# Edge weights loaded pair by pair, edge attributes in 1 KB rows, and an activation written with a step that restores the order of edges

## The chip, the core and the metric

The kernel runs on one core of one Trainium2 chip. The metric is the device time of one execution in microseconds (us); the lower, the better. The core has five engines that work side by side: TensorE (PE, matrix products; its weight loads are listed as PEld), VectorE (DVE), ScalarE (ACT), GpSimd (POOL) and SyncE (SP), which here issues nearly all plain DMAs. Sixteen DMA engines move the data. In the profile, SPq is SP's queue of instructions.

## What is computed

One layer of graph attention with 12,500 nodes of 128 channels and 400,000 edges, sorted by their destination. The edges' part is what the change touches:

```python
msg_src = node_input @ w_src + b_src
msg_dst = node_input @ w_dst
message = msg_src[edge_src] + msg_dst[edge_dst]
rad_w = silu(silu(edge_scalars @ w1 + b1) @ w2 + b2) @ w3 + b3     # 32 -> 64 -> 64 -> 128
message = message * edge_attr * rad_w                              # edge_attr: one weight per edge
message = message @ w_sep + b_sep
alpha, value = halves of each of 8 heads                           # 16 + 16 channels a head
score = sum(smooth_leaky_relu(alpha) * alpha_dot)                  # one per edge and head
att = softmax of score over the edges of one destination
out = segment_sum(value * att, edge_dst) @ w_proj + b_proj
```

The layer's input is a normalized and rectified `x`, and `x` is added to its output. `edge_scalars` is the input `edge_attr_32` (32 numbers per edge, the *attributes*), and `edge_attr` is the input `edge_weight1` (the *weight* of an edge). All numbers are 32-bit floats.

## The kernel before

**Stages.** A first stage makes the two tables of node messages, `t_src` and `t_dst`, in DRAM. The main stage, `passes`, walks over the edges. A last stage projects the sums and adds `x`. The change lies in `passes` alone.

**Sections and pairs.** The edges are cut into 800 sections of `SEC = 500` (four tiles of `T = 125`), and two consecutive sections make a pair of `PR = 1000`. There are `NP = 400` pairs. One call of `step(k)` does one piece of the work of several pairs at once: loads for pairs ahead, the radial net and the message of pair k, and the sums of the older pair `c = k - LAG`, with `LAG = 12`. The order inside a step is written by hand (`manual_schedule`), and each engine takes its own instructions in that order.

**The radial net.** `load_e(g)` brings the attributes of four pairs (500 KB) into the tile `e_t`, every fourth step. Edge number j·125 + p of the group goes to partition p, column block j, so each DMA row is one edge's 32 floats, 128 bytes. `e_T` transposes a pair on PE, and ACT copies the result to `eT`. `mlp1` and `mlp2` are matrix products, each followed by a SiLU on ACT (L740, L755). Blocks on the diagonal of the weights let one product treat two sets of edges. `mlp3` (L769) has PE form the 128 radial factors of the 1000 edges in PSUM, and DVE adds the bias and multiplies with the edge weights, giving two tiles `rad` (L772).

**The weights.** `load_w(g)` broadcasts the weights of two pairs (2000 floats) to all 128 partitions, 1000 KB in all, into `w_b` with two buffers. It is called at every even step, for the pairs k + 2 and k + 3.

**The message.** `message` adds, on PE, the transposed gathered rows `gs` (L782) and a product of a one-hot matrix with `m3` (L788). `m3` holds `md`, the rows of `t_dst` that the pair needs, split into three bf16 parts by `split_md`; the first part is a cast on ACT (L704), and `md` is loaded by `load_md(k + 3)` (L698). DVE multiplies by `rad` to get `mT` (L793). `alphas` (L797, L799, L801), `scores` and the softmax come after that. The rows `gs` are gathered by POOL (L718), eight indirect DMAs a step.

**The sums.** `sums(c)` leaves the sums of pair c in `ob` (ACT, L896). `store(c, f)` writes 63 rows of them to `agg` in DRAM at a place that is read from a register (L903). Because those places are not known beforehand, each store to `agg` waits until the store before it has landed.

**SP's queue.** SP issues in the order of the calls. In a step this is: `store_win` in one step of four, the first store of pair c - 1, `load_w` in even steps, two `md` loads, in steps with k % 4 == 1 the loads `d_b` (L687, the local destination numbers of four pairs, 500 KB) and `e_t` (L681), and then the second store of pair c - 1. Traffic of scores and of the softmax comes at the end of some steps.

Of the kernel before, what the change touches and what calls it, by code (L numbers as in the profile page):

```python
# [21 lines left out]
F32 = mybir.dt.float32  # L22
# [3 lines left out]
ALU = mybir.AluOpType  # L26
# [4 lines left out]
P = 128  # L31
C = 128
H = 8
RAD = 32
# [11 lines left out]
T = 125  # L46
TS = 4
SEC = T * TS
W = 64
PR = 2 * SEC  # L50
# [6 lines left out]
def gnn_kernel(ctx: ExitStack, tc: tile.TileContext, a: dict, out: bass.AP):  # L57
    nc = tc.nc
    x, src, dst = a["x"], a["src"], a["dst"]
    ea, ew = a["edge_attr_32"], a["edge_weight1"]  # L60
# [84 lines left out]
    with tc.tile_pool(name="node", bufs=2) as np_, tc.tile_pool(name="node1", bufs=1) as n1, \  # L145
# [27 lines left out]
        w3, b3 = load("fc_w3", [FC, C]), load("fc_b3", [C, 1])  # L173
# [463 lines left out]
    def passes(w1b, w2b, w3b, b12, w_s, b_s, row, far):  # L637
        src_t = src.rearrange("(s e) -> s e", e=SEC)
        dst_t = dst.rearrange("(s e) -> s e", e=SEC)
        ea_t = ea.rearrange("(g j p) c -> g p j c", j=32, p=T)  # L640
        ew_p = ew.rearrange("(g e) o -> o g e", e=2 * PR)
        with tc.tile_pool(name="wk2", bufs=2) as sp, tc.tile_pool(name="ps", bufs=1, space=PSUM) as pp, \
                tc.manual_schedule(), ExitStack() as held:
            lp = held.enter_context(tc.tile_pool(name="ld", bufs=2))
            prep, e_g, d_g, w_g, md, gath = {}, {}, {}, {}, {}, {}
            eTs, h1s, h2s, ohT, m3, mr, mTs, als, S_all, sms, Ps, Pem, pvx, ohs, accs, Sps, Ms = (
                {} for _ in range(17))
# [29 lines left out]
                prep[u] = (idx, loc)  # L677

            def load_e(g):
                e_g[g] = lp.tile([T, 32, RAD], F32, name="e_t")  # L680
                nc.sync.dma_start(out=e_g[g], in_=ea_t[g])  # L681

            def load_d(g):
# [2 lines left out]
                at = bass.AP(at.tensor, at.offset, [[NP * SEC, 2], [0, W], [1, 4 * SEC]])  # L686
                nc.sync.dma_start(out=d_g[g].rearrange("p k e -> p (k e)"), in_=at)  # L687

            def load_w(g):
                w_g[g] = lp.tile([P, 2, PR], F32, name="w_b")  # L690
                nc.sync.dma_start(out=w_g[g].rearrange("p k e -> p (k e)"),
                                  in_=ew_p[:, g, :].to_broadcast([P, 2 * PR]))

            def load_md(k):
                md[k] = lp.tile([P, C], F32, name="md", bufs=4)
                at = [nc.sync.value_load(base[0:1, f, k:k + 1]) for f in range(2)]
                for f in range(2):
                    nc.sync.dma_start(out=md[k][f * W:(f + 1) * W, :], in_=t_dst[ds(at[f], W), :])  # L698
# [23 lines left out]


            def e_T(k):
                ev = e_g[k // 4].rearrange("p (k f t) c -> p k f (t c)", k=4, f=2)
                pe = pp.tile([P, 2, T], F32, name="m1")
                for g in range(2):
                    nc.tensor.transpose(pe[:, g, :], ev[:, k % 4, g, :], ident[:T, :T])
                eTs[k] = sp.tile([P, 2 * T], F32, name="eT")
                nc.scalar.copy(eTs[k], pe.rearrange("p g e -> p (g e)"))  # L730
# [13 lines left out]
            def mlp2(k):  # L744

                p2 = pp.tile([P, 2, BANK], F32, name="p3")
                h1 = h1s.pop(k)
                for h in range(2):
                    s = slice(h * FC, (h + 1) * FC)
                    for f in range(2):  # L750
                        o = slice(f * FC, (f + 1) * FC)
                        nc.tensor.matmul(p2[o, h, 0:2 * T], w2b[s, o], h1[s, f * 2 * T:(f + 1) * 2 * T],  # L752
                                         start=True, stop=True)
                h2s[k] = sp.tile([P, SEC], F32, name="h2")
                nc.scalar.activation(h2s[k].rearrange("x (q h p) -> x h q p", q=2, h=2),  # L755
                                     p2[:, :, 0:2 * T].rearrange("x h (q p) -> x h q p", q=2),
                                     AF.Silu, bias=b12[:, 1:2], scale=1.0)

# [6 lines left out]
            def mlp3(k):  # L765
                p3 = pp.tile([C, 2, BANK], F32, name="p3")
                for f in range(2):
                    s = slice(f * FC, (f + 1) * FC)
                    nc.tensor.matmul(p3[:, f, 0:SEC], w3b[s, :], h2s[k][s, :], start=True, stop=True)  # L769
                rads = [sp.tile([C, SEC], F32, name="rad", bufs=3) for _ in range(2)]  # L770
                for f in range(2):
                    nc.vector.scalar_tensor_tensor(  # L772
                        rads[f], p3[:, f, 0:SEC], b3, w_g[k // 2][:, k % 2, f * SEC:(f + 1) * SEC],
                        op0=ALU.add, op1=ALU.mult)
                return rads

            def message(k, rads):
                gs = gath[k]
                pm = [pp.tile([C, SEC], F32, name="pm", bufs=2) for _ in range(2)]
                for f in range(2):  # L780
                    for t in range(TS):
                        nc.tensor.matmul(pm[f][:, t * T:(t + 1) * T], gs[:T, f * TS + t, :],  # L782
                                         ident[:T, :T], start=(t == 0), stop=False,
                                         is_transpose=True, skip_group_check=True)
                for j in range(3):
                    for f in range(2):
                        s = slice(f * W, (f + 1) * W)
                        nc.tensor.matmul(pm[f], m3[k][s, j, :], ohT[k][s, :], start=False, stop=(j == 2),  # L788
                                         skip_group_check=True)
                mTs[k] = sp.tile([C, PR], F32, name="mT", bufs=LAG + 1)  # L790
                for f in range(2):
                    s = slice(f * SEC, (f + 1) * SEC)
                    nc.vector.tensor_mul(mTs[k][:, s], pm[f], rads[f])  # L793

            def alphas(k, f):
                pa = pp.tile([C, SEC], F32, name="pa")
# [101 lines left out]
            def store_win(g):  # L898
                nc.sync.dma_start(out=win[4 * g:4 * g + 4].rearrange("k p c -> p k c"), in_=accs[g])
# [5 lines left out]
            def has(k):  # L905
                return 0 <= k < NP
# [5 lines left out]
            def step(k):  # L912
                c = k - LAG
                if has(c - 1):
                    if c % 4 == 0:
                        store_win(c // 4 - 1)
                    store(c - 1, 0)

                if k % 16 == 4 and has(k + 12):
                    prep_load((k + 12) // 16)  # L920
                if k % 2 == 0 and has(k + 2):
                    load_w((k + 2) // 2)
                if has(k + 3):
                    load_md(k + 3)
                if k % 4 == 1 and has(k + 3):
                    load_d((k + 3) // 4)
                if k % 4 == 1 and has(k + 7):
                    load_e((k + 7) // 4)
                if has(k + 4) and (k + 4) % MP == 0:
                    load_sm((k + 4) // MP)  # L930
                if has(c - 1):
                    store(c - 1, 1)
                if 0 <= 2 * k < NZ:
                    for i in range(2 * k, min(2 * k + 2, NZ)):
                        zero(i)
                if k % 16 == 8 and has(k + 8):
                    prep_make((k + 8) // 16)
                if has(k + 4):
                    gather(k + 4)
                if has(k + 1):  # L940
                    split_md(k + 1, 0)
                if has(c):
                    sums_begin(c)
                if has(k):
                    message(k, mlp3(k))
                if has(c):
                    values(c, 0)
                if has(k + 1):
                    split_md(k + 1, 1)
                if has(k):  # L950
                    alphas(k, 0)
                if has(k + 1):
                    split_md(k + 1, 2)
                if has(k + 2):
                    mlp1(k + 2)
                if has(c):
                    values(c, 1)
                if has(k):
                    alphas(k, 1)
                if has(k + 1):  # L960
                    mlp2(k + 1)
                    one_hot_T(k + 1)
                    split_md(k + 1, 3)
                if has(c):
                    sums(c)
                m, r = divmod(k, MP)
                if has(k - MP):
                    if r == 1:
                        softmax_up(m - 1)
                    elif r == 2:  # L970
                        softmax_down(m - 1)
                        softmax_exp(m - 1)
                    elif r == 3:
                        softmax_T(m - 1)
                if has(k + 3):
                    e_T(k + 3)
                if has(k) and k % 2 == 1:
                    scores(k)
# [137 lines left out]
            q = P // 4  # L1116
# [143 lines left out]
```

## Time and profile before

| | |
|---|---|
| median of 13 runs | 5404.36 us (5388.98 to 5413.15) |
| the profiled execution | 5396.09 us, of which the profile spans 5394.1 us |
| mean granted TensorE clock | 0.909 |
| busy share of the span | PE 82%, PEld 46%, DVE 56%, ACT 36%, POOL 58% |
| DMA | 796441 packets, 732.97 MB; 500482 packets under 512 B |
| first and last start of the products L769 | 232.9 and 5127.1 us after the span's start |

The time is nearly all in the 400 steps between those two starts. A line of the profile's groups reads: line, engine, operation, output<-inputs, shapes, number of instructions | busy time in us, mean of one in ns | idle time of the engine just before them and what ended it. A line of the waits reads: engine, line and tile that waited, what it waited for, total us, times, longest. A line of the timeline reads: start, length, engine, line, operation and tiles, and how many instructions were merged. SP's instructions only issue DMAs and are not counted as busy in the page; its timeline shows them.

### The profile page before, as it was taken

How to read it: one execution, taken by the hardware profiler on the slowest of the kernel's cores; microseconds unless marked ns; L12 is line 12 of the kernel's file. 1: busy time of each engine (PE TensorE's matmuls, PEld its weight loads, DVE VectorE, ACT ScalarE, POOL GpSimd, SP SyncE). 2: the span in 40 equal slices, each digit the busy share in tenths (PEclk: the TensorE clock that was granted, in tenths of full speed). 3: DMA queues.
4: the chain of work that ended last, by engine and by line, in shares of the span. 5: the costliest groups of instructions: out<-in, count | busy, mean ns of one | idle time of the engine just before them, and what ended most of it. 6: DMA issues, size and time to landing. Idle time of an engine off the chain costs nothing. (4 is left out here: it accounts for less than half of the span.)

```text
span 5394.1 us, 85488 instructions
## 1 busy us (share of the span) xinstructions
PE 4434.7 (82%) x29840; PEld 2478.3 (46%) x29840; DVE 3040.6 (56%) x6033; ACT 1920.9 (36%) x4597; POOL 3117.4 (58%) x3231
## 2 busy tenths in 40 slices
PE   3478889888888888888888888889888988898855
PEld 2224444444444444444444444444444544444444
DVE  5235555555555555555555555556555655555556
ACT  2233333333433333333333333333333433333311
POOL 0266566666665666666666666666566665666511
PEclk7689999999999999999999999999999999999975
DMA  3355555555555555555555555555555555555522
GB/s 136 107 151 141 140 132 138 143 142 133 137 143 140 130 139 146 142 134 142 138 142 144 133 135 142 138 135 139 141 140 136 138 144 140 132 138 144 128 76 115
DMA packets 796441, 732.97 MB, mean 136 GB/s; under 512 B 500482, under 2 KB 697578, under 8 KB 795748
## 3 DMA queue, kind: packets, MB, share of 16 engines
q1 hardware_dynamic: 689980, 510.07, 31.5%
q0 software_dynamic: 102816, 210.37, 20.3%
q10 hardware_dynamic: 3202, 6.99, 0.3%
q8 instruction: 235, 3.85, 0.3%
q14 instruction: 208, 1.70, 0.1%
HBM read 592.44 MB, written 135.07 MB: 135 GB/s over the span
## 5 line engine op out<-in xcount | busy, mean ns | idle before, releaser
L718 POOL DMA_INDIRECT gs<-t_src,idx x3200 | 3074.9, 961 | 2020.8 <-PE pm L782 911.2
L797 PE MATMUL pa<-mT,c_w_a 128*128 128x500 f32 x1600 | 931.4, 667 | 626.7 <-DVE mT L793 560.7
L799 ACT ACTIVATE sl<-pa,c_b_a 128x500 f32<-128x500 f32 x800 | 541.6, 677 | 1781.6 <-PE pa L797 1781.1
L772 DVE SCALAR_TENSOR_TENSOR rad<-p,c_fc_b,w_b 128x500 f32<-128x500 f32 x800 | 553.3, 733 | 964.6 <-DMA w_b<-in_edge_weight 774.8
L801 DVE SCALAR_TENSOR_TENSOR al<-pa,sl 128x500 f32<-128x500 f32 x800 | 543.0, 679 | 797.4 <-ACT sl L799 766.7
L880 PE MATMUL V<-c_w_v,mT 128*125 128x128 f32 x6208 | 947.6, 299 | 0.1
L880 PEld LDWEIGHTS V<-c_w_v,mT 128*125 128x125 f32 x6208 | 794.1, 200 | 310.2 <-issue 209.0
L882 DVE TENSOR_TENSOR pvx<-V,Pem 125x512 f32<-125x512 f32 x776 | 532.0, 686 | 204.7 <-PE V L880 204.7
L797 PEld LDWEIGHTS pa<-mT,c_w_a 128*128 128x128 f32 x1600 | 265.3, 208 | 676.5 <-DVE mT L793 594.8
L793 DVE TENSOR_TENSOR mT<-pm,rad 128x500 f32<-128x500 f32 x800 | 504.1, 672 | 89.4 <-PE pm L788 89.0
L891 PE MATMUL misc<-pvx,oh 125*64 125x136 f32 x6400 | 468.3, 287 | 27.4 <-DVE pvx L882 27.0
L782 PEld LDWEIGHTS pm<-ident,gs 125*128 125x128 f32 x3200 | 342.2, 143 | 300.8 <-issue 299.4
L769 PE MATMUL p<-h,w3b 64*128 64x500 f32 x1600 | 450.5, 640 | 1.9 <-ACT h L755 1.9
L891 PEld LDWEIGHTS misc<-pvx,oh 125*64 125x64 f32 x6400 | 362.8, 137 | 178.4 <-issue 177.7
L782 PE MATMUL pm<-ident,gs 125*128 125x125 f32 x3200 | 435.5, 280 | 0.0
L704 ACT CAST m<-md 128x128 bf16<-128x128 f32 x400 | 118.8, 297 | 765.6 <-DMA md<-t_dst 765.6
L788 PE MATMUL pm<-ohT,m 64*128 64x500 bf16 x2400 | 324.3, 376 | 6.0 <-DVE ohT L762 6.0
L737 PE MATMUL p<-eT,w1b 64*128 64x250 f32 x1600 | 318.9, 480 | 1.0 <-ACT eT L730 1.0
L737 PEld LDWEIGHTS p<-eT,w1b 64*128 64x128 f32 x1600 | 136.8, 209 | 345.1 <-issue 343.4
L740 ACT ACTIVATE h<-p,b 128x500 f32<-128x500 f32 x400 | 272.2, 681 | 22.5 <-PE p L737 22.4
L755 ACT ACTIVATE h<-p,b 128x500 f32<-128x500 f32 x400 | 269.4, 674 | 3.3 <-PE p L752 3.3
L867 DVE TENSOR_TENSOR oh<-lane,loc 125x504 f32<-125x504 f32 x400 | 269.2, 673 | 0.0
(148 smaller groups left out, 3386.7 us busy)
## 6 DMA issues: line engine op xcount, KB each, us to landing
w_b<-in_edge_weight SPq DMA_DIRECT2D x200, 1000.0 KB
gs<-t_src,idx POOLq DMA_INDIRECT x3200
e_t<-in_edge_attr SPq DMA_DIRECT2D x100, 500.0 KB
d_b<-loc_d SPq DMA_DIRECT2D x100, 500.0 KB
sc_d<-Sp SPq DMA_DIRECT2D x100, 500.0 KB
win<-ob SPq DMA_DIRECT2D x100, 272.0 KB
agg<-ob SPq DMA_DIRECT2D x800, 33.5 KB
md<-t_dst SPq DMA_DIRECT2D x800, 32.0 KB
```

The source lines that it names most:

```text
L718: nc.gpsimd.indirect_dma_start(out=gs[:, j, :], out_offset=None, in_=t_src[:, :], in_offset=bass.IndirectOffsetOnAxis(ap=idx[:, t:t + 1], ...
L737: nc.tensor.matmul(p1[:, q, 0:2 * T], w1b[s, :], eTs[k][s, :], start=True, stop=True)
L769: nc.tensor.matmul(p3[:, f, 0:SEC], w3b[s, :], h2s[k][s, :], start=True, stop=True)
L772: nc.vector.scalar_tensor_tensor(rads[f], p3[:, f, 0:SEC], b3, w_g[k // 2][:, k % 2, f * SEC:(f + 1) * SEC], op0=ALU.add, op1=ALU.mult)
L782: nc.tensor.matmul(pm[f][:, t * T:(t + 1) * T], gs[:T, f * TS + t, :], ident[:T, :T], start=(t == 0), stop=False, is_transpose=True, skip_ ...
L793: nc.vector.tensor_mul(mTs[k][:, s], pm[f], rads[f])
L797: nc.tensor.matmul(pa, w_a, mTs[k][:, f * SEC:(f + 1) * SEC], start=True, stop=True)
L799: nc.scalar.activation(sl, pa, AF.Silu, bias=b_a, scale=1.0)
L801: nc.vector.scalar_tensor_tensor(al, pa, 0.25, sl, op0=ALU.mult, op1=ALU.add)
L880: nc.tensor.matmul(V[:, t, :], mTs[c][:, o:o + T], w_v, start=True, stop=True)
L882: nc.vector.tensor_mul(pvx[c][:, f, :, 0:C].rearrange("p t (h k) -> p t h k", h=H), V.rearrange("p t (h k) -> p t h k", h=H), Pem[c // MP] ...
L891: nc.tensor.matmul(acc[f * W:(f + 1) * W, :], ohs[c][:, f * TS + t, :], pvx[c][:, f, t, :], start=(t == 0), stop=(t == TS - 1), skip_group ...
```

## The change

Four things are edited, all in `passes`.

1. **Weights by the pair.** `load_w(k)` loads one pair (500 KB) into one of four buffers, and is called in every step for pair k + 3, ahead of `load_md`. There are 400 loads in the place of 200, with the same bytes.
2. **Attributes in 1 KB rows.** Partition p now takes eight consecutive edges of a pair, p·8 to p·8 + 7. A DMA row is 8·32 floats, 1024 bytes; 500 rows in the place of 4000 for the same 500 KB, once in four steps as before.
3. **Second activation.** The edges come out of `mlp2` in the order of that layout. The SiLU of `mlp2` writes its output with a step of four floats, so that `h2` holds, for one half of each partition's eight edges, the edges in order (column 4p + r).
4. **Radial factors.** The two DVE instructions of `mlp3` write into one tile `rad` of 1000 columns, each in runs of four floats with a step of eight, and read the weights in the same pattern. `message` reads two contiguous halves of that tile. It has one buffer in place of three half-sized ones.

The number and the sizes of PE, DVE and ACT instructions are as before.

```diff
-        ea_t = ea.rearrange("(g j p) c -> g p j c", j=32, p=T)
-        ew_p = ew.rearrange("(g e) o -> o g e", e=2 * PR)
+        ea_t = ea.rearrange("(g k p r) c -> g p k (r c)", k=4, p=T, r=8)
+        ew_p = ew.rearrange("(k e) o -> o k e", e=PR)
...
-                e_g[g] = lp.tile([T, 32, RAD], F32, name="e_t")
+                e_g[g] = lp.tile([T, 4, 8 * RAD], F32, name="e_t")
                 nc.sync.dma_start(out=e_g[g], in_=ea_t[g])
...
-            def load_w(g):
-                w_g[g] = lp.tile([P, 2, PR], F32, name="w_b")
-                nc.sync.dma_start(out=w_g[g].rearrange("p k e -> p (k e)"),
-                                  in_=ew_p[:, g, :].to_broadcast([P, 2 * PR]))
+            def load_w(k):
+                w_g[k] = lp.tile([P, PR], F32, name="w_b", bufs=4)
+                nc.sync.dma_start(out=w_g[k], in_=ew_p[:, k, :].to_broadcast([P, PR]))
...
-                ev = e_g[k // 4].rearrange("p k (f t) c -> p k f (t c)", k=4, f=2)
+                ev = e_g[k // 4].rearrange("p k (g c) -> p k g c", g=2)
...
-                nc.scalar.activation(h2s[k].rearrange("x (q h p) -> x h q p", q=2, h=2),
+                nc.scalar.activation(h2s[k].rearrange("x (p q h) -> x h q p", q=2, h=2),
...
-                rads = [sp.tile([C, SEC], F32, name="rad", bufs=3) for _ in range(2)]
+                rad = sp.tile([C, PR], F32, name="rad", bufs=1)
                 for f in range(2):
                     nc.vector.scalar_tensor_tensor(
-                        rads[f], p3[:, f, 0:SEC], b3, w_g[k // 2][:, k % 2, f * SEC:(f + 1) * SEC],
-                        op0=ALU.add, op1=ALU.mult)
-                return rads
+                        rad.rearrange("x (p f r) -> x f p r", f=2, r=4)[:, f], p3[:, f, 0:SEC].rearrange("x (p r) -> x p r", r=4), b3,
+                        w_g[k].rearrange("x (p f r) -> x f p r", f=2, r=4)[:, f], op0=ALU.add, op1=ALU.mult)
+                return rad
...
-                    nc.vector.tensor_mul(mTs[k][:, s], pm[f], rads[f])
+                    nc.vector.tensor_mul(mTs[k][:, s], pm[f], rad[:, s])
...
-                if k % 2 == 0 and has(k + 2):
-                    load_w((k + 2) // 2)
                 if has(k + 3):
+                    load_w(k + 3)
                     load_md(k + 3)
```

More of the change, by code (lines that the diff above doesn't have):

```diff
@@ L724, in e_T @@
             def e_T(k):
-                ev = e_g[k // 4].rearrange("p (k f t) c -> p k f (t c)", k=4, f=2)
+                ev = e_g[k // 4].rearrange("p k (g c) -> p k g c", g=2)
                 pe = pp.tile([P, 2, T], F32, name="m1")
@@ L769, in mlp3, with message @@
                     nc.tensor.matmul(p3[:, f, 0:SEC], w3b[s, :], h2s[k][s, :], start=True, stop=True)
-                rads = [sp.tile([C, SEC], F32, name="rad", bufs=3) for _ in range(2)]
+                rad = sp.tile([C, PR], F32, name="rad", bufs=1)
                 for f in range(2):
                     nc.vector.scalar_tensor_tensor(
-                        rads[f], p3[:, f, 0:SEC], b3, w_g[k // 2][:, k % 2, f * SEC:(f + 1) * SEC],
-                        op0=ALU.add, op1=ALU.mult)
-                return rads
-            def message(k, rads):
+                        rad.rearrange("x (p f r) -> x f p r", f=2, r=4)[:, f], p3[:, f, 0:SEC].rearrange("x (p r) -> x p r", r=4), b3,
+                        w_g[k].rearrange("x (p f r) -> x f p r", f=2, r=4)[:, f], op0=ALU.add, op1=ALU.mult)
+                return rad
+            def message(k, rad):
                 gs = gath[k]
```

## The prediction

> **What bounds the kernel now.** I first read who waited for whom.
>
> ```profile
> DVE rad L772 <- DMA w_b<-in_edge_weight: 774.8, 98, 17.3
> ACT m L704 <- DMA md<-t_dst: 765.6, 101, 21.3
> PE pa L797 <- DVE mT L793: 560.7, 156, 14.2
> ```
>
> Two loads come late some 100 times, once in four steps, and PE then waits for the message. That the weights are late invites the reading that they are asked for too late. So I read who makes SP late, in SP's own waits.
>
> ```profile
> SPq L903 <- DMA agg<-ob: 495.7, 321, 11.3
> SPq L820 <- DMA sc_d<-Sp: 139.0, 50, 12.0
> ...
> SPq L903 <- ACT ob L896: 12.4, 6, 5.7
> ```
>
> SP waits for its own transfers, and hardly ever for a compute engine (ob: 12.4 us in all). A queue that never waits for the others is itself the pace. Its timeline over one round of four steps shows where the round goes:
>
> ```profile
> 2630.96 0.61 SPq L687 DMA_DIRECT2D d_b<-loc_d  x1
> 2631.68 0.38 SPq L681 DMA_DIRECT2D e_t<-in_edge_attr  x1
> 2632.89 21.93 SPq L903 DMA_DIRECT2D agg<-ob  x2
> 2654.86 0.38 SPq L691 DMA_DIRECT2D w_b<-in_edge_weight  x1
> 2656.27 1.19 SPq L698 DMA_DIRECT2D md<-t_dst  x2
> ...
> 2679.97 0.38 SPq L681 DMA_DIRECT2D e_t<-in_edge_attr  x1
> 2681.54 22.07 SPq L903 DMA_DIRECT2D agg<-ob  x2
> ```
>
> From one blocked store to the next is 2681.54 - 2632.89 = 48.65 us, or 12.16 a step; the kernel's mean step, from the first and last start of L769, is (5127.1 - 232.9)/399 = 12.27. SP's round is the kernel's round. Of it, 21.9 us are two stores right behind d_b and e_t. The issue of the first is held (its line says so: 307/335/20866 ns as least, median and longest), and the second waits until the first has landed.
>
> ```profile
> 2632.00:2644.00 12.00, 12.00 (x90) 6.72 (x86) 9.33 (x19) 6.16 (x14) 9.23 (x10) 1.00 0.56 117
> 2644.00:2653.50 9.50, 7.50 (x56) 4.58 (x54) 6.17 (x13) 4.74 (x11) 7.21 (x8) 1.00 0.36 81
> ```
>
> These are two stretches of the block (last column GB/s, the one ahead the DMA share). By the trace's packet records, the first carries d_b (128 packets of 4000 bytes, about 11 a us) and 2400 of e_t's 4000 packets of 128 bytes, about 260 a us. The second carries the other 1600 at about 178 a us, with the DMA engines 36% busy: 3 : 2, as if five DMA engines held 800 rows each and two of these had to finish d_b first. The store's last rows follow the last 128-byte packet within 0.5 us, and SP goes on 0.5 us later. So the tail of e_t lies wholly on SP's path: 9.3 us a round, from 2644.1 to 2653.4.
>
> **The floor below SP.** Steps without a late load start L769 every 9.30 us (2681.88 to 2691.18), 10.36 with scores (2671.52 to 2681.88), 13.83 with the exponentials (2641.33 to 2655.16), and 12.23 where the next block of indices is made (once in 16). With the late steps put at 9.30, eight steps make 4 x 9.30 + 2 x 10.36 + 13.83 + (10.36 + 12.23)/2 = 83.05, or 10.38 a step. POOL's gathers need (3074.9 + 841.3)/400 = 9.79, below that.
>
> **The change, part by part**, per round of four steps on SP's path:
>
> *1 KB rows.* On the two slow DMA engines, 800 rows at 9.3/800 = 11.6 ns each become 100 rows. The trace has no 1024-byte row in this load, but the 1002-byte rows of `sm` take 46 ns (median; mean 53), and the 544-byte rows of the stores follow each other at 25 ns, or 47 per KB. 100 x 46.5 ns = 4.65 us: saved 4.65. The ends: at the mean of 53 ns plus a tenth for the gathers beside it, 5.8 us, saved 3.5; at the 4000-byte packets' best rate (156 ns) 4.0 us, saved 5.3. [...] d_b, the first 11.5 us of the block, is not touched.
>
> *Weights by the pair.* Two more issues a round at 0.38 to 0.40 us each stand in SP's queue ahead of md and the second store: +0.78. The half-sized load ahead of a store may let it land sooner: 0 to 0.5 gained, counted as 0. The longer lead is worth nothing by itself: md(k + 3) has the same lead as before, it is queued behind the weights, and it was late as often (101 and 98 times) by nearly as much. After the change the wait at L772 goes, and the wait at L704 stays.
>
> *The second activation.* No ScalarE row writes with a 16-byte step, so its cost is bounded. From below: none, 674 ns as now (L755); a gain is excluded, as the elements are as many. From above, the nearest row is DVE's:
>
> ```profile
> L676 DVE COPY loc<-misc 125x128 f32<-125x128 f32 x25 | 9.6, 383 | 0.0
> L1163 DVE COPY v_out<-pv 128x128 f32<-128x128 f32 x1 | 0.3, 292 | 0.9 <-PE pv L1161 0.9
> ```
>
> Both copy 128 floats from PSUM; L676 writes with a step of four floats, and costs 91 ns more, 0.71 an element. For 500: +355 ns, so 1.03 us, and I take that value. [...] In plain steps PE comes to the next mlp3 about 0.6 us after h2 is done (L755 ends at 2640.72, L769 starts at 2641.33), which hides it. In odd steps ACT's copy of ob comes 0.35 later, and the scores (L808) wait for that: 4 x 0.35 in eight steps, a floor of 84.4, or 10.56 a step. SP's round hides this; without that cover it costs 0.35 x 200 = 70 us.
>
> *rad.* Runs of four floats: writes with every second float (L1064, 681 to 693 ns for 512) cost no more than contiguous ones (L1212, 692), so 733 ns stays. From above, L676's 0.71 on both instructions, 0.71 us a step, which DVE has ahead of mT: the floor of eight steps would be 84.4 + 5.7 = 90.1 at most, level with SP's two rounds below. PE's instructions do not change; one buffer for rad costs nothing, as DVE runs rad and mT in order.
>
> **Sum.** -4.65 + 0.78 = -3.87 us a round. SP's round becomes 48.65 - 3.9 = 44.8, or 11.2 a step, still above the floor of 10.56, so SP keeps the pace. Some 97 of the 100 rounds are paced so: -3.87 x 97 = -375. Against the profiled execution: 5396 - 375 = 5021. The median of the runs lies 8 us above that execution: 5030. The case's own range: saved 3.5 to 5.3 on the tail and 0 to 0.5 on the stores, less 0.78, is 2.7 to 5.0 a round, 260 to 490 us, or 4915 to 5140.
>
> **Rivals.** *A, the lead frees the loop.* If SP's round falls below the floor (say the store no longer stands behind e_t once its issue is not held), steps take 10.56: (12.27 - 10.56) x 390 = 667 saved, 4737. For it: two wait lines name the loads. Against: a store ends with nine completion packets, and in the trace the last two come only after e_t, so it lands no sooner than e_t however early it is issued. Chance 0.09.
>
> *B, the strided writes become the pace.* If ACT's penalty is several times L676's and rad pays too, a step takes 11.4 to 12.2 us: 5100 to 5400. Against: L676 and L1064. Chance 0.14, of which a little is no gain or worse.
>
> *C, slower: bytes, not rows, set e_t's tail.* If a 1 KB row costs what eight small rows cost, the tail stays 9.3 us, and the two extra issues are all that remains: +0.78 x 97 = 76, 5480. It decides from 8.5 us a tail, 85 ns a row. Against: no row of about 1 KB took that long. Chance 0.06.
>
> **How the numbers follow.** The forecast has 0.71. The range reaches from 4915 up through most of B, to 5270; A, C and the end of B are left out, 0.2 together. Faster by over 0.2% (11 us, about what a measurement of this kernel can tell from no change): 0.71 + 0.09 + 0.10 = 0.90; within it 0.02; slower 0.02 + 0.06 = 0.08.
>
> **What would show it.** Right: the block behind e_t is 17 to 18 us long, SP's round 44 to 46, L772's wait for w_b near zero while L704 still waits 200 to 450 us for md; L755 near 1.0 us, L772 at 733 ns; packets down by 350,000 less 0 to 2%. Wrong: SP waiting for ob (the floor rules, A or B, told apart by L755 and L772), or a block of still 21 us (C).

## The result, and the profile after

The changed kernel takes 5086.82 us (median of 8 runs, 5079.38 to 5100.33), the kernel before 5403.79 in all its runs so far. The ratio is 0.9421, with a 95% interval of 0.9409 to 0.9433: 317 us less, where 374 had been forecast. The profiled execution took 5082.5 us with a span of 5080.5, against 5396.09 and 5394.1 before; its mean granted TensorE clock is 0.928, against 0.909.

SP's timeline of one round shows again what sets the pace (start, length, line, DMA, how many merged):

```profile
2607.81 0.62 SPq L687 DMA_DIRECT2D d_b<-loc_d  x1
2608.53 0.39 SPq L681 DMA_DIRECT2D e_t<-in_edge_attr  x1
2609.76 19.20 SPq L902 DMA_DIRECT2D agg<-ob  x2
2629.00 0.37 SPq L691 DMA_DIRECT2D w_b<-in_edge_weight  x1
2630.41 1.19 SPq L697 DMA_DIRECT2D md<-t_dst  x2
...
2653.81 0.49 SPq L681 DMA_DIRECT2D e_t<-in_edge_attr  x1
2655.15 18.80 SPq L902 DMA_DIRECT2D agg<-ob  x2
```

The two stores behind e_t now hold SP 18.8 to 19.2 us in the place of 21.9, and from one such block to the next it is 2655.15 - 2609.76 = 45.4 us in the place of 48.65. The two stretches of this block, with the clock granted to PE, the DMA engines' busy share and GB/s in the last columns:

```profile
2609.00:2621.50 12.50, 12.49 (x101) 6.94 (x104) 8.00 (x15) 6.22 (x14) 9.45 (x11) 1.00 0.53 116
2621.50:2628.00 6.50, 6.17 (x40) 2.90 (x32) 4.53 (x9) 0.83 (x2) 4.98 (x6) 1.00 0.31 93
```

The first stretch, in which d_b flows, is as long as before. The second, the end of e_t alone, has become shorter. The granted clock is 1.00 in these stretches, as it was in those of the block before, so the shorter block is not the clock's work. The waits of the compute engines:

```profile
ACT m L703 <- DMA md<-t_dst: 859.7, 178, 15.9
...
DVE rad L771 <- PE p L768: 415.1, 328, 3.3
...
PE pa L796 <- DVE al L800: 326.4, 139, 8.1
...
DVE mr L706 <- ACT m L703: 287.0, 81, 11.3
```

DVE no longer waits for the weights at all (774.8 us before). ACT waits for md, and longer than before (765.6), and DVE waits 287.0 us for the ACT instruction that this holds up. SP's own waits are of the same kind as before:

```profile
SPq L902 <- DMA agg<-ob: 959.7, 358, 11.7
SPq L819 <- DMA sc_d<-Sp: 149.2, 50, 11.7
...
SPq L902 <- ACT ob L895: 7.0, 8, 2.4
```

SP waits 7.0 us in all for ob at that line: it is still the pace, for itself. Two groups carry the stepped writes; here are their lines before and then after:

```profile
L772 DVE SCALAR_TENSOR_TENSOR rad<-p,c_fc_b,w_b 128x500 f32<-128x500 f32 x800 | 553.3, 733 | 964.6 <-DMA w_b<-in_edge_weight 774.8
L755 ACT ACTIVATE h<-p,b 128x500 f32<-128x500 f32 x400 | 269.4, 674 | 3.3 <-PE p L752 3.3
...
L771 DVE SCALAR_TENSOR_TENSOR rad<-p,c_fc_b,w_b 128x500 f32<-128x500 f32 x800 | 553.1, 733 | 415.3 <-PE p L768 415.1
L754 ACT ACTIVATE h<-p,b 128x500 f32<-128x500 f32 x400 | 475.6, 1189 | 18.8 <-PE p L751 18.8
```

rad costs 733 ns as before; the second activation went from 674 to 1189 ns.

### The profile page after: what moved, and what is told of

Same layout as the page of the kernel before. It is cut to its first block, busy times and chain, and to the rows that moved or that the text cites. A ratio compares the mean times of both kernels' runs of the same rounds, so it can differ in the third digit from the quotient of the medians.

```text
span 5080.5 us, 85841 instructions
## 1 busy us (share of the span) xinstructions
PE 4365.5 (86%) x29840; PEld 2439.1 (48%) x29840; DVE 3065.6 (60%) x6033; ACT 2073.2 (41%) x4597; POOL 3139.7 (62%) x3231
## 5 line engine op out<-in xcount | busy, mean ns | idle before, releaser
L796 PE MATMUL pa<-mT,c_w_a 128*128 128x500 f32 x1600 | 883.7, 635 | 371.3 <-DVE al L800 326.4
L879 PE MATMUL V<-c_w_v,mT 128*125 128x128 f32 x6208 | 884.6, 285 | 0.1
L879 PEld LDWEIGHTS V<-c_w_v,mT 128*125 128x125 f32 x6208 | 736.6, 187 | 288.2 <-issue 190.7
L890 PE MATMUL misc<-pvx,oh 125*64 125x136 f32 x6400 | 504.5, 302 | 25.3 <-DVE pvx L881 24.9
L890 PEld LDWEIGHTS misc<-pvx,oh 125*64 125x64 f32 x6400 | 393.8, 146 | 193.0 <-issue 192.4
L754 ACT ACTIVATE h<-p,b 128x500 f32<-128x500 f32 x400 | 475.6, 1189 | 18.8 <-PE p L751 18.8
L703 ACT CAST m<-md 128x128 bf16<-128x128 f32 x400 | 118.8, 297 | 860.2 <-DMA md<-t_dst 859.7
L706 DVE TENSOR_TENSOR mr<-md,m 128x128 f32<-128x128 f32 x400 | 113.8, 285 | 287.7 <-ACT m L703 287.0
L751 PE MATMUL p<-h,w2b 64*64 64x250 f32 x3200 | 285.1, 429 | 0.8 <-ACT h L739 0.8
L736 PE MATMUL p<-eT,w1b 64*128 64x250 f32 x1600 | 279.1, 426 | 1.0 <-ACT eT L729 1.0
L739 ACT ACTIVATE h<-p,b 128x500 f32<-128x500 f32 x400 | 272.6, 681 | 0.8 <-PE p L736 0.7
```

Source lines behind the costliest of these rows:

```text
L754: nc.scalar.activation(h2s[k].rearrange("x (p q h) -> x h q p", q=2, h=2), p2[:, :, 0:2 * T].rearrange("x h (q p) -> x h q p", q=2), AF.Si ...
L796: nc.tensor.matmul(pa, w_a, mTs[k][:, f * SEC:(f + 1) * SEC], start=True, stop=True)
L879: nc.tensor.matmul(V[:, t, :], mTs[c][:, o:o + T], w_v, start=True, stop=True)
L890: nc.tensor.matmul(acc[f * W:(f + 1) * W, :], ohs[c][:, f * TS + t, :], pvx[c][:, f, t, :], start=(t == 0), stop=(t == TS - 1), skip_group ...
```

## The experiments

The theory of the prediction: SP's round sets the pace, and the gain is the shortened end of the attribute load, behind which a store stands (theory of the tail). The rival: the weights were asked for too late, and the longer lead brings the gain.

Kernels e1 to e4 ran together on one chip, where the kernel before took 5411.39 us. Each ratio is to the kernel before on the same chip. For comparison, this table has SP's round of four steps and its block (from the issue of the store right behind e_t to the issue of the next store), as means over 256 pairs of steps in each trace:

| kernel | time, us | ratio to before (95%) | block, us | round, us |
|---|---|---|---|---|
| before | 5404 | | 21.9 | 48.84 |
| changed | 5087 | 0.9421 (0.9409, 0.9433) | 18.8 | 45.87 |
| e1: weights alone | 5391 | 0.9955 (0.9938, 0.9972) | 21.8 | 48.86 |
| e2: rows alone | 5174 | 0.9569 (0.954, 0.9599) | 18.6 | 46.64 |
| e3: changed, d_b split | 4678 | 0.8641 (0.8627, 0.8655) | 9.2 | 41.79 |
| e4: changed, d_b and e_t from ACT's queue | 4717 | 0.8722 (0.8707, 0.8736) | 6.1 | 41.82 |
| h1: before, d_b split | 4690 | 0.8656 (0.8638, 0.8673) | 11.7 | 41.70 |

**e1, the weights alone.** The kernel before with this edit only:

```diff
-        ew_p = ew.rearrange("(g e) o -> o g e", e=2 * PR)
+        ew_p = ew.rearrange("(k e) o -> o k e", e=PR)
...
-            def load_w(g):
-                w_g[g] = lp.tile([P, 2, PR], F32, name="w_b")
-                nc.sync.dma_start(out=w_g[g].rearrange("p k e -> p (k e)"),
-                                  in_=ew_p[:, g, :].to_broadcast([P, 2 * PR]))
+            def load_w(k):
+                w_g[k] = lp.tile([P, PR], F32, name="w_b", bufs=4)
+                nc.sync.dma_start(out=w_g[k], in_=ew_p[:, k, :].to_broadcast([P, PR]))
...
-                        rads[f], p3[:, f, 0:SEC], b3, w_g[k // 2][:, k % 2, f * SEC:(f + 1) * SEC],
+                        rads[f], p3[:, f, 0:SEC], b3, w_g[k][:, f * SEC:(f + 1) * SEC],
...
-                if k % 2 == 0 and has(k + 2):
-                    load_w((k + 2) // 2)
                 if has(k + 3):
+                    load_w(k + 3)
```

> The kernel before, with the weights by the pair, three steps ahead, and nothing else. Theory of the tail (SP's round is the pace; the gain comes from the end of the attribute load behind which a store stands): SP gets two more issues a round and nothing off, so the round goes from 48.8 us to 48.9 to 49.6 and the time from 5404 to between 5415 and 5480; the wait of rad for the weights disappears and the wait of the md cast stays or grows. Rival (the weights were asked for too late): most of the 317 us of the whole change shows here, 5090 to 5200.

Measured: 5391.0, a ratio of 0.9955, some 20 us gained, where the theory had expected 10 to 75 us lost and the rival 200 or more gained. The wait for the weights is gone, and this one has taken its place:

```profile
ACT m L703 <- DMA md<-t_dst: 1107.3, 162, 21.6
```

SP's round is what it was (48.86): where a load of weights stands ahead of a store, the next store follows 1.0 us sooner a round (the two places take 5.1 us in all, 6.1 before), and the other intervals, two of which have one more issue, grew by as much. The profiled execution spans 5395.7 us, level with the 5394.1 of the profile before, which is not one of this chip's runs; where the 20 us of the medians lie is not seen. Here the longer lead of a load that came late because its issuer was late moved the wait to the next load in that issuer's queue: rad's 774.8 us for the weights went, and the 765.6 of ACT for md became 1107.3. The rival falls as the main cause.

**e2, the rows alone.** The changed kernel with the weights as before (not shown here: `load_w` itself and its use in `mlp3`, also as before):

```diff
...
-                if has(k + 3):
-                    load_w(k + 3)
+                if k % 2 == 0 and has(k + 2):
+                    load_w((k + 2) // 2)
```

> The changed kernel with the weights as before (two pairs at once, at even steps, two buffers): attributes in 1 KB rows, stepped activation and the one rad tile alone. Theory of the tail: the block of stores shrinks by about 3.1 us as in the full change, SP's round is 45.7, the time 5070 to 5130, although rad still waits for the weights some 100 times. Rival (lead of the weights): within 30 us of the kernel before, 5404.

Measured: 5173.91. The block shrank as expected, to 18.6 us, and three quarters of the gain are here, with the late loads still late:

```profile
ACT m L704 <- DMA md<-t_dst: 564.3, 104, 17.4
DVE rad L772 <- DMA w_b<-in_edge_weight: 467.4, 65, 14.4
```

But the time is 44 us above the expected range, and the two parts alone (0.45% and 4.3%) do not add up to the 5.8% of both. Outside the block, the round takes 46.64 - 18.6 = 28.0 us, against 27.1 in the changed kernel. Where the 1000 KB of weights stand ahead of a store, the next store follows after 3.5 to 3.6 us (mean of the two places in a round), in the changed kernel after 2.4 to 2.6. That is 2 us a round, and two more issues and longer intervals elsewhere take back about 1.3. So the halved loads seem to pay because stores land sooner behind them. That is read from the intervals and not shown: a run with the short lead and half-sized loads was not made.

**e3, d_b in two loads.** Left in the block is d_b. Its source's outermost step has two entries, and by the prediction's reading two DMA engines carry it all: in the block of the profile before, its 128 rows of 4000 bytes add up to 21.9 us and fill 12.5 us, 1.8 at a time. That two loads of 64 rows would take more engines was an estimate that no trace had shown. The edit, in the changed kernel:

```diff
-                at = loc_d[0:1, 4 * g, :]
-                at = bass.AP(at.tensor, at.offset, [[NP * SEC, 2], [0, W], [1, 4 * SEC]])
-                nc.sync.dma_start(out=d_g[g].rearrange("p k e -> p (k e)"), in_=at)
+                for f in range(2):
+                    at = loc_d[f:f + 1, 4 * g, :]
+                    at = bass.AP(at.tensor, at.offset, [[0, W], [1, 4 * SEC]])
+                    nc.sync.dma_start(out=d_g[g][f * W:(f + 1) * W].rearrange("p k e -> p (k e)"), in_=at)
```

> The changed kernel with the load d_b made as two loads of 64 rows each (one per half) instead of one load whose outermost step has two entries. Theory of the tail: d_b is the first 13 us of what a store waits for, because two DMA engines carry all of it; spread over more engines it takes 2 to 3 us, the block falls from 18.8 to 7 to 9 us, SP's round to 35 to 36 us, below the floor of the compute engines (about 42 us for four steps), so the compute engines take over the pace at 10.4 to 10.6 us a step: 4690 to 4790; SP then waits for ob. Rival (the load stays on two engines, or the bytes themselves set the block): no gain, and one issue more, 5087 to 5150.

Measured: 4677.95, with the same bytes and one issue more a round. SP's timeline:

```profile
2643.98 1.24 SPq L688 DMA_DIRECT2D d_b<-loc_d  x2
2645.32 0.45 SPq L681 DMA_DIRECT2D e_t<-in_edge_attr  x1
2646.51 9.39 SPq L903 DMA_DIRECT2D agg<-ob  x2
2655.99 0.37 SPq L692 DMA_DIRECT2D w_b<-in_edge_weight  x1
```

The block is 9.2 us in the mean, and SP now waits for a compute engine, which it hardly did before (8.5 us in all at that line):

```profile
SPq L903 <- DMA agg<-ob: 1048.5, 336, 9.9
SPq L815 <- ACT pvx L863: 489.2, 92, 8.9
```

The starts of mlp3 on PE have no late steps left:

```profile
2605.71 1.11 PE L769 MATMUL p<-h,w3b 64*128 64x500 f32 x4
2615.01 1.11 PE L769 MATMUL p<-h,w3b 64*128 64x500 f32 x4
2629.04 1.11 PE L769 MATMUL p<-h,w3b 64*128 64x500 f32 x4
2638.34 1.11 PE L769 MATMUL p<-h,w3b 64*128 64x500 f32 x4
```

They are 9.30 and 14.03 us apart. Over 360 steps the mean is 10.46, which is the floor of the compute engines. This version beats both kernels. The DMA packets agree with the reading of two engines: e3 has 3000 more packets of 4 bytes than the changed kernel (such as the completion packets of the prediction, nine a store), 30 for each of the 100 loads, as if two DMA engines had become twice sixteen.

**e4, another queue.** In the changed kernel, the same two loads come from ScalarE's queue:

```diff
-                nc.sync.dma_start(out=e_g[g], in_=ea_t[g])
+                nc.scalar.dma_start(out=e_g[g], in_=ea_t[g])
...
-                nc.sync.dma_start(out=d_g[g].rearrange("p k e -> p (k e)"), in_=at)
+                nc.scalar.dma_start(out=d_g[g].rearrange("p k e -> p (k e)"), in_=at)
```

> The changed kernel with d_b and the attributes issued from ScalarE's queue instead of SP's; same loads, same rows. Theory of the tail: the store waits because it is queued behind these two loads on the same queue; on another queue it lands within about 3 us, the block goes, SP's round falls to about 30 us and the compute engines rule: 4690 to 4800, with two issues on ScalarE in four steps (some 0.5 us each) as the only addition. Rival (the DMA engines themselves are full of these loads, whatever queue they come from): the block stays near 19 us and the time near 5087.

Measured: 4717.18. Nothing about the loads is changed but the queue, and the block falls to 6.1 us. So the store's place in the queue held it, and the rival (5087) falls. A part of the hold remains, beside the store: the intervals ahead of it and behind it grew from 5.1 and 3.6 to 7.0 and 7.3 us.

```profile
SPq L902 <- DMA agg<-ob: 1408.6, 490, 9.5
```

SP waits longer for landing stores than in any of the runs above, but it does not cost time here: the round is e3's. The 39 us to e3 lie ahead of step 16, whose mlp3 starts at 450.1 us, against 409.8 in e3. ACT's two issues cost it 0.51 us each.

**f1, is the change needed at all?** The kernel before, with e3's edit and nothing of the change.

> The kernel before, with d_b made as two loads of 64 rows each and nothing else (attributes in 128-byte rows, weights as before). Theory of the tail: the block behind d_b and e_t is then only the attributes' part, 800 rows an engine at 11.6 ns = 9.3 us and about 3 us of landing, so 12 to 13 us in the place of 21.9; SP's round goes to 39 to 41 us, just under the floor of 41.5, and the time to 4650 to 4800, without any part of the change. Rival (the 128-byte rows hold the loop wherever they are): 4950 or more.

This run, f2, f3 and f4 fell on another chip, where the kernel before takes 7333.23 us. There ACT stands idle for over a millisecond ahead of the second activation (1087.4 us in f1), for something that the trace has no releaser for ("remote" below). SP is then not the pace (in the repeat it waits 1298.8 us for ACT before it stores the scores), and forecasts made for 5404 do not apply. f1 took 7050.28, a ratio of 0.9613 (0.9599, 0.9628). A repeat, g1, fell on a second chip of that kind (7336.85 for the kernel before): 7048.88, 0.9606 (0.9587, 0.9625).

> The kernel before with d_b made as two loads of 64 rows each and nothing else, once more, as the chip of the last four runs took 7333 us for the kernel before itself. On a chip where the kernel before takes about 5404: theory of the tail: SP's round falls to 39 to 41 us, under the floor of the compute engines (10.38 a step), and the time to 4650 to 4800, without any part of the change. Rival (the 128-byte rows hold the loop wherever they are): 4950 or more.

A second repeat, h1, ran on a chip where the kernel before takes 5422.67.

> The kernel before with d_b made as two loads of 64 rows each and nothing else, for a chip on which the kernel before takes about 5404. There the block behind d_b and e_t should be 11 us as on the slower chip (it is the DMA engines' time), SP's round 48.8 - 10.9 + 0.6 = 38.5 us, under the floor of the compute engines of 41.5, and the time 4650 to 4720, level with the changed kernel with the split load (4678) or a little below it, since the second activation is at 674 ns. Rival (the 128-byte rows hold the loop wherever they are): 4950 or more. On a chip that takes about 7300 for the kernel before: 7050 again.

Measured: 4689.99, inside the expected range. SP's timeline, with the 128-byte rows still in place:

```profile
2652.09 1.23 SPq L688 DMA_DIRECT2D d_b<-loc_d  x2
2653.43 0.44 SPq L681 DMA_DIRECT2D e_t<-in_edge_attr  x1
2654.67 11.05 SPq L904 DMA_DIRECT2D agg<-ob  x2
```

The block is 11.7 us, and the round 41.7 us: level with the compute engines. Here too there are 3000 more packets of 4 bytes than in the kernel before. The ratios of e3 and h1 to the kernel before overlap. With d_b split, the whole change is worth nothing that these runs can tell.

**f2, the attributes over more DMA engines.** The changed kernel with e_t in two loads:

```diff
-                nc.sync.dma_start(out=e_g[g], in_=ea_t[g])
+                for p0, p1 in ((0, 120), (120, T)):
+                    nc.sync.dma_start(out=e_g[g][p0:p1], in_=ea_t[g][p0:p1])
```

> The changed kernel with the attribute load made as two loads, of 120 and of 5 partitions. Theory of the tail with five engines: 125 rows are split over five DMA engines only, 120 can go over fifteen; the end of e_t behind d_b falls from 5.6 us to 2 us, one issue (0.4 us) is added, the block is 15 to 15.8 us, SP's round 42.3 to 43, about level with the compute engines: 4740 to 4870. Rival (the load's end is set by rows or bytes whatever their number of partitions): 5087 to 5130.

Measured, on the slower chip: 7455.58, a ratio of 1.0177 (1.0161, 1.0192). The time decides nothing. The timelines of f2 and, below it, of f4 (e_t in one load; but for md's lead it is the changed kernel), on the same chip:

```profile
3529.05 2.70 SPq L682 DMA_DIRECT2D e_t<-in_edge_attr  x2
3532.57 13.30 SPq L903 DMA_DIRECT2D agg<-ob  x2
```

```profile
3533.70 0.39 SPq L681 DMA_DIRECT2D e_t<-in_edge_attr  x1
3535.34 17.49 SPq L902 DMA_DIRECT2D agg<-ob  x2
```

From the first issue of e_t to the end of the block it is 16.8 us against 19.1. The means over the loads of the middle of the kernel agree (16.8 and 19.0), and f2 has 1500 more packets of 4 bytes than f4, 15 a load, as if five DMA engines had become fifteen and five. The direction is that of the theory; the size is about two thirds of the 3.4 us that were expected. That 120 rows would go over fifteen engines was an estimate that no earlier run had shown.

**f3, the second activation without its step.** e3 with

```diff
-                nc.scalar.activation(h2s[k].rearrange("x (p q h) -> x h q p", q=2, h=2),
+                nc.scalar.activation(h2s[k].rearrange("x (q h p) -> x h q p", q=2, h=2),
```

> The changed kernel with the split d_b, and the second activation written without the step (contiguous runs of 125), so that the edges of a pair come out in another order than the weights and messages; all else the same. It prices the stepped write where SP does not cover it. By the prediction's term the odd steps lose 0.35 us each to it, 70 us in all: against 4678 with the step, 4608 without. By the steps seen in the run with the step (10.36 in odd steps as before the change, only the step with the exponentials at 14.03 in the place of 13.83) it is 0.2 us once in eight steps, 10 us: 4660 to 4675. The activation itself should go from 1189 to about 675 ns.

Its output is not the layer's, as edges and weights no longer match. Measured, on the slower chip: 7052.41, a ratio of 0.9607 (0.9593, 0.9621), the same as f1. It could not price the step in the kernel's time there, as no run with the step and the split load fell on that chip. The activation itself takes 679 ns, and 1142 with the step in f4 on the same chip: the step alone makes it dearer.

**f4, more lead for md.** The changed kernel with five buffers of md and

```diff
-                    load_md(k + 3)
+                if has(k + 4):
+                    load_md(k + 4)
```

> The changed kernel with md loaded four steps ahead instead of three (five buffers), so that md too has a longer lead. Theory of the tail: SP's round sets the pace and no lead changes it: within 20 us of 5087, the late load being whatever SP issues last. Rival (a lead is what is missing, and after the weights md is the next late one): the md wait of 860 us goes, the time falls by 150 to 350 us, to 4740 to 4940.

Its three runs (f4, g2, h2) all fell on these slower chips: 1.0188 (1.0172, 1.0203), 1.0186 (1.0166, 1.0207) and 1.0239 (1.0209, 1.0268).

> The changed kernel with md loaded four steps ahead instead of three (five buffers), once more for the same reason. Theory of the tail: SP's round sets the pace and no lead changes it: within 20 us of 5087. Rival (a lead is what is missing, and after the weights md is the next late one): the md wait of 860 us goes and the time falls to 4740 to 4940.

> The changed kernel with md loaded four steps ahead instead of three (five buffers), for a chip on which the kernel before takes about 5404. Theory of the tail: SP's round sets the pace and no lead changes it: within 20 us of 5087, the late load being whatever SP issues last. Rival (a lead is what is missing, and after the weights md is the next late one): the md wait of 860 us goes and the time falls to 4740 to 4940. On a chip that takes about 7300 for the kernel before: about 7470 again.

On the faster chips it is therefore untested. What the slower chips do to ACT, from g2, by the second activation's own list of idle time (us, times):

```profile
  remote: 1130.7, 298
  PE m L727: 58.2, 28
```

The mean granted TensorE clock of g2 is 0.797, against 0.928 in the changed kernel; whether that is a cause of the idle time or comes of it is not shown. The changed kernel itself was not run on these chips, and why ACT stands still there stays open.

## Why the prediction was right, step by step

**The bound.** Right. SP's round was the kernel's round before (48.84 us for four steps of 12.21) and after (45.87 for four of 11.47), and e3, e4 and h1 show what happens when it is not: steps at the floor. My sign for it was weaker than I took it to be. Only in e3 does SP then wait for ACT (489.2 us); at the same line it is 52.3 us in e4 and 32.8 in h1. So a queue that does not wait for the others need not be the pace; the step lengths decide.

**The end of e_t.** The mechanism was right, the size too large. By the trace's packet records, the last rows that the two slow DMA engines carry took 9.22 us in the mean before and 5.93 after: 59 ns a row of 1 KB, where I had put 46.5. So 3.3 us were saved, and 3.1 of them show in the block, not 4.65; the block is 18.8 us long, where I had put 17 to 18. Half of the 1 KB rows take 47 ns or less, as I had priced them; but the last 200 of a load take 49.7 in the mean, and the other 9 of the 59 ns are not in the rows' own durations. What fills them is not shown (the gathers run beside these rows). My worse end, the mean of the 1002-byte rows with a tenth on top, gave 5.8 and came nearest. With 100 rows on each of the two, 102,400 bytes in 5.93 us are an estimated 17 GB/s an engine.

**The weights.** Priced at +0.78 us a round, and it was nearly nothing: outside the block the round grew by 0.1 us (48.84 - 21.9 = 26.9 before, 45.87 - 18.8 = 27.1 after). The stores behind the halved loads follow sooner by 1.1 us a round (the two places take 5.0 us in all, 6.1 before), which I had counted as 0 of a possible 0.5, a guess that rested on no run.

**The sum.** -3.87 a round predicted, -2.97 measured; times 97, 288 us. Most of the rest of the 314 us between the two spans, about 24, came off the first 16 steps (mlp3 of step 16 starts at 456.8 us before and 433.1 after). I had not counted these. That the sum came so near is partly luck: the saving at the tail lies below the 3.5 to 5.3 us that I had allowed, the issues cost 0.7 us less than I had put, and the 24 us helped too.

**The second activation.** I took 0.71 ns an element from DVE's copy, 1.03 us in all; it is (1189 - 674)/500 = 1.03 ns an element, 1.19 us in all. That copy (L676) was right in direction for a write of single floats, and too small in size; rad's runs of four floats cost nothing (733 ns before and after). That it is hidden was right, and more fully than I said: steps with scores stay at 10.36 us, and only those with the exponentials go from 13.83 to 14.03. The floor with it is 10.46 a step (e3), not 10.56: where SP does not cover it, the step costs 0.2 us once in eight steps, an estimated 10 us in all, and not 70.

**Where the late loads show.** I expected L703 to wait 200 to 450 us for md; it was 859.7. That idle time need not be what the kernel loses: DVE waited only 287.0 us for that cast. Why it grew so much is not shown. The packets fell by 321,000, not by 343,000 to 350,000, as I had left out that twice as many weight loads are twice as many packets.

**The rivals.** A asked that the store no longer stand behind e_t. In the change it still did. In e3 it stands behind loads that end much sooner, and in e4 behind neither of them; SP's round falls to the floor in both, and they reach 4678 and 4717, close to the 4737 that A would have given. B did not come: the stepped write was dearer than I took, but covered. C did not come: a row cost 59 ns on the tail, below the 85 from which it decides. Single rows of about 1 KB had taken longer than that before (286 of the 6400 of 1002 bytes, the longest 495 ns), which I had denied; their mean was 53.

**How many DMA engines d_b fills.** The packet records name no engine; the two, five and nine are read from the 4-byte packets, as one for each engine that a transfer uses. In the block of the profile before, three of these start at 2642.2 to 2642.9, and no 128-byte row starts from there to 2644.5. Two start at 2644.5 and 2644.8, where d_b's last rows start (2644.6), eleven at 2653.2 to 2654.0, at the end of e_t and of the first store, and nine at 2655.7 to 2655.9, behind the second store. So a store (63 rows) has nine, d_b two and e_t (125 rows) five. The other records agree: e_t's rows in the ratio 3 : 2 over the two stretches, 30 more 4-byte packets a load when d_b is split (2 to 16 + 16), 15 more when e_t is (5 to 15 + 5), and the block of 9.2 us in e3. What sets these numbers is not shown.

## What to carry to other kernels

When a load is late, ask first whether its issuer is: read the issuing queue's own waits and timeline, and compare its round with the kernel's. Where the queue was the pace, as here, lead and buffers moved the wait to the next load (e1: 1107.3 us for md). Then look in that queue for what a small transfer with a dependence (here a store that the next store waits for) stands behind. How a load is divided can matter more than the length of its rows: here the split of d_b into two loads gained 13% (h1, 0.8656), and beside it a change that had gained 6% (0.9421) was worth nothing that the runs can tell (e3, 0.8641).

## What the runs showed of the hardware

A DMA issue was itself held: over the middle of the kernel, the store behind e_t took 19.7 us to issue in the mean with 128-byte rows, 11.1 with 1 KB rows, 9.5 in h1 (128-byte rows, d_b split), and 0.5 in e3 (1 KB rows, d_b split). On ScalarE, the second activation's write with a step of 16 bytes cost 1.03 ns an element more than the one in contiguous runs before (1189 and 674 ns for 500 elements a partition). And two of the chips ran the kernel before in 7130 to 7337 us (medians), where the others took 5404 to 5423; the runs that were profiled there have ACT idle where the trace shows no cause.
